# A transformer block with attention and routed experts on one core: pair results in three buffers with a later scatter, a last part reordered around residuals read from PSUM, and early finishing in five steps

## The chip, the core and the metric

The kernel runs on one core of a Trainium2 chip. A core has five engines with queues of their own: TensorE (matmul, "PE"; its weight loads are listed as "PEld"), VectorE ("DVE"), ScalarE ("ACT"), GpSimd ("POOL") and SyncE ("SP", which here only issues DMAs). ACT and POOL issue DMAs too. Each engine works through its instructions in order and waits on semaphores for the others. Matmul results go to PSUM[...]. The metric is device time in microseconds, the median over runs of the same program.

## The reference

The input x has 8 sequences of 512 tokens with 256 features, all fp32. First attention (4 groups of 4 query heads, head size 128, causal), then a feed-forward layer with 64 routed experts and one shared expert. Both are wrapped in layer norms and added to the residual:

```python
x = x + _layernorm(attn(_layernorm(x), wq, bq, wkv, bkv, wo))
x = x + _layernorm(ffn(_layernorm(x), gate_w, w_gate, w_up, w_down, sh_gate, sh_up, sh_down))

# ffn: logits -> softmax -> the best 6 of 64 experts per token
# each expert takes its first 64 tokens, in token order over all sequences
g = silu(einsum('ech,ehf->ecf', buf, w_gate)); u = einsum('ech,ehf->ecf', buf, w_up)
d = einsum('ecf,efh->ech', g * u, w_down)
y = weighted sum of d over the chosen experts
y = y + (silu(x @ sh_gate.T) * (x @ sh_up.T)) @ sh_down.T
```

An expert has 256 inputs and 176 hidden values, the shared expert 352 hidden values. An expert's 64 places are mostly taken by the first sequences.

## The kernel before

The order of instructions on each engine is written out by hand: the Python code emits them in the order in which each engine will do them.

**Attention.** 128 head steps, k = 16 b + s (sequence b, head s). In a step TensorE does the scores of head k (`psc`), the output projection of head k-3 (`po`, accumulated in two PSUM banks o0 and o1 over a sequence), the queries of head k+1 (`pq`, which DVE turns into `qt`) and the mix of head k-2 (`pav`, which ACT copies to `ao`). Between scores and mix, DVE takes the row minimum, ACT the exponential (`e`), DVE the reciprocal of the sum, POOL the multiplication with it ("weigh", L306), DVE and two DMA legs through DRAM the transposition (`eb` to `ex_d` to `et`).

**Feed-forward of sequence b** rides along in sequence b+1's head steps, at fixed places. A place is a letter in the head step: A after weigh, B after the projection, M after the queries, D after the mix. The dictionary `steps` in `feed_forward` names head and place ("7A"). `shared` is the shared expert as a generator: hidden values in three chunks of 128, 128 and 96 columns, taken in the order 2, 1, 0, each as matmuls into two banks (`psg`, `psu`), a tanh on ACT (`gs`) and two DVE operations (`hid`, L692 and L693), and then the 12 products with `sd_sb` (L698). `route` is the router, `output` the last layer norm and residual of a sequence.

**Experts.** The first five sequences (EARLY) write their normalised rows to DRAM. From the end of sequence 5 on, `experts` works off 32 pairs of experts, two calls per pair step, up to four calls per head step: gather of rows by an indirect DMA of POOL (`gx`), weights (`wgu`, `wd`) by DMAs that ACT issues, `gate_up`, `turn_hidden`, `down`. `down` has ACT scale the bank `pd` into `dd` (L584), and POOL scatters `dd` into `y_d` in DRAM with an adding indirect DMA (L585). `dd` comes from a pool of two buffers. Tokens of sequences 5 to 7 that an expert still takes are handled by the "late" pair, with 0/1 matrices instead of an indirect DMA.

**Early finishing.** When all pairs are done, `finish_early` finishes sequences 0 to 4, one step per head step from head 5 of sequence 7 on, at the place before `queries` (L927). `finish` issues two loads of `y_d` and one of the residual `x1_d` from SP, then adds the two (L661, DVE) and goes on into `output`: statistics, scaling on ACT, residual add on POOL, store. A new sequence starts every second step.

**The end.** After head 127, `last_part` does the feed-forward of sequence 7, which nothing rides along with, and in between what is left of sequence 6 (`shared6`, `output6`) and of the early finishing (`spare`). The PSUM banks are three of tag "s", three of tag "m", and o0 and o1.

Of the kernel before, what the change touches and what calls it, by code (L numbers as in the profile page):

```python
# [11 lines left out]
F32 = mybir.dt.float32  # L12
# [32 lines left out]
def sandwich_kernel(ctx, tc, x, wq, bq_t, wkv, bk_t, bv, wo, gate_wt, w_gate, w_up, w_down,  # L45
# [77 lines left out]
    with ExitStack() as part:  # L123
# [446 lines left out]
        def down(key):  # L570
            l = pairs[key] if key == "late" else pairs.pop(key)
            pd = ps_m.tile([P, E], F32, tag="m", name=f"pd_{key}")
            for c in range(2):
                for e in range(2):
                    nc.tensor.matmul(pd[ts(e, CAP), :], lhsT=l["ht"][:, c, ts(e, CAP)],
                                     rhs=l["wd"][:, e, c, :], start=c == 0, stop=c == 1)
            dd = p3.tile([P, E], F32, tag="dd", name=f"dd_{key}")
            if key == "late":
                l["dd"] = dd
                on_act(dd, pd)  # L580
                return
            for e in range(2):
                rows = slice(e * CAP, (e + 1) * CAP)
                nc.scalar.mul(dd[rows, :], pd[rows, :], l["gw"][rows, e : e + 1])  # L584
            nc.gpsimd.indirect_dma_start(  # L585
                out=y_d[:, :], out_offset=bass.IndirectOffsetOnAxis(ap=table["idx"][:, key, 1:2], axis=0),
                in_=dd, in_offset=None, compute_op=ALU.add)
# [32 lines left out]
        def experts():  # L620


            yield from tables()
            yield
            yield from free_slots()
            yield
            for m in range(NM + 5):
                if m < NM:
                    start_pair(m)
                for behind_, step in ((5, down), (3, gate_up), (4, turn_hidden), (2, turn_rows),  # L630
                                      (1, load_gate_up), (3, load_down)):
                    if 0 <= m - behind_ < NM:
                        step(m - behind_)
                yield
                if 0 <= m - 3 < NM:
                    gate_up_hidden(m - 3)
                if m == NM + 4:
                    pairs["all"] = True
                yield
# [14 lines left out]
        def finish(b, tags):  # L654

            ys = [q.tile([P, NI, E], F32, tag=tag, name=f"y{n}_{b}") for n, (q, tag) in enumerate(tags[:2])]
            for k in range(2):
                nc.sync.dma_start(out=ys[k], in_=rows_of(y_d, k * (ET_ROWS + CAP) + b * T))
            x1 = residual(b, *tags[2])
            yield  # L660
            nc.vector.tensor_add(ys[0], ys[0], ys[1])  # L661
            yield from output(b, ys[0], x1)
# [6 lines left out]
        def shared(b, xt2, l, banks="mmmmmm"):  # L669

            hid = p1.tile([P, len(SH_CHUNKS), T], F32, tag="hid", name=f"hid_{b}")
            banks = iter(banks)

            for n, (f0, fw) in reversed(list(enumerate(SH_CHUNKS))):
                mw = min(P, fw + NX // 2)
                pgu = []
                for w_sb, name in ((sg_sb, "psg"), (su_sb, "psu")):
                    tag = next(banks)
                    pp = {"m": ps_m, "s": ps_s}[tag].tile([P, T], F32, tag=tag, name=f"{name}_{b}_{n}")
                    for c in range(NC):  # L680
                        nc.tensor.matmul(pp[:mw, :], lhsT=w_sb[:, c, ds(f0, mw)], rhs=xt2[:, c, :],
                                         start=c == 0, stop=c == NC - 1)
                    pgu.append(pp)
                if fw < P:
                    l["lg"] = p1.tile([NX, T], F32, tag="y", name=f"lg_{b}")
                    on_act(l["lg"][: NX // 2, :], pgu[0][fw:, :])
                    on_act(l["lg"][NX // 2 :, :], pgu[1][fw:, :])

                gs = p2.tile([P, T], F32, tag="gs", name=f"gs_{b}_{n}", bufs=1)
                nc.scalar.activation(gs[:fw, :], pgu[0][:fw, :], AF.Tanh, scale=0.5)  # L690
                yield
                nc.vector.scalar_tensor_tensor(gs[:fw, :], gs[:fw, :], 1.0, pgu[0][:fw, :], ALU.add, ALU.mult)  # L692
                nc.vector.scalar_tensor_tensor(hid[:fw, n, :], gs[:fw, :], 0.5, pgu[1][:fw, :], ALU.mult, ALU.mult)  # L693
                yield
# [6 lines left out]
            if b == B - 1:  # L701
                l["py"] = [ps_o.tile([P, 2, E], F32, tag=f"o{n}", name=f"py_{b}_{n}") for n in range(2)]
                for i in range(NI):
                    products(i, l["py"][i // 2][:, i % 2, :], i % 2 == 0, False)
                yield
                return
# [14 lines left out]
        def feed_forward(b):  # L721
# [79 lines left out]

            steps["shared"], steps["output"] = go("f"), lambda: next(l["out"]) if "out" in l else begin_output()
            return steps

        def last_part(before, spare):
# [4 lines left out]
            shared6, output6 = before["shared"], before["output"]  # L810
            shared6()
            mv, rs = norm_scales([sums[i // 2][:, i % 2, :] for i in range(NI)], f"o{b}")
            shared6()
            shared6()
            shift = shifts(mv, rs, f"o{b}")
            two = p2.tile([P, 2, NI * E], F32, tag="v", name="o_xt2")
            o, xt2 = two[:, 0].rearrange("p (i e) -> p i e", i=NI), two[:, 1].rearrange("p (c t) -> p c t", c=NC)
            st = small.tile([P, NI, 6], F32, tag="st", name=f"st_f{b}")
            for i in range(NI):
                scale_on_act(o[:, i, :], sums[i // 2][:, i % 2, :], rs, shift, i)  # L820
                nc.vector.tensor_add(xt[:, i, :], xt[:, i, :], o[:, i, :])
                nc.vector.bn_stats(st[:, i, :], xt[:, i, :])
            mv, rs = scales_of(st, NI, f"f{b}")
            shared6()
            shift = shifts(mv, rs, f"f{b}")
            nc.sync.dma_start(out=rows_of(x1_d, b * T), in_=xt)
            xg = p1.tile([P, NI, ROW], F32, tag="xg", name=f"xg_{b}")
            for i in range(NI):
                if i % 2:
                    scale_on_act(xg[:, i, :E], xt[:, i, :], rs, shift, i)  # L830
                else:
                    normalize(xg[:, i, :E], xt[:, i, :], mv, rs, i)
            transpose_rows(xt2, xg, f"f{b}")
            f = shared(b, xt2, l, "msmsms")
            next(f)
            r = route(b, xg, l)
            for _ in spare:
                pass
            next(r)
            shared6()  # L840
            next(r)
            next(r)
            next(r)
# [5 lines left out]
            next(f)  # L849
            gate_up("late")  # L850
            next(f)
            gate_up_hidden("late")
            next(f)
            turn_hidden("late")
            next(f)
            down("late")
            py = l["py"]
# [3 lines left out]
            shared6()  # L861
            output6()
            output6()
# [5 lines left out]
            shift = shifts(mv, rs, f"y{b}")  # L869
            for i in range(NI):  # L870
                scale_on_act(o[:, i, :], py[i // 2][:, i % 2, :], rs, shift, i)
                nc.vector.tensor_add(xt[:, i, :], xt[:, i, :], o[:, i, :])  # L872
                if i % 2:
                    nc.sync.dma_start(out=rows_of(out, b * T)[:, i - 1 : i + 1, :], in_=xt[:, i - 1 : i + 1, :])
            output6()
# [4 lines left out]
        def finish_early():  # L880
            rows = [finish(b, EARLY_TAGS + [[(p1, "xn"), (p2, "xnt")][b % 2]]) for b in range(EARLY)]
            yield
            for t in range(2 * EARLY + 2):
                for b in range(EARLY):
                    if 0 <= t - 2 * b < 4:
# [22 lines left out]
        for k in range(NK):  # L908
# [50 lines left out]
            if twice and not finishing:  # L959
                next(routed, None)  # L960
# [92 lines left out]
```

## Time and profile before

| what | us |
|---|---|
| median of 3 runs (1465.49 to 1471.9) | 1470.83 |
| the profiled execution | 1466.5 |
| its span, first to last instruction | 1464.8 |
| TensorE busy / DVE / ACT / POOL | 1405.2 / 890.4 / 509.7 / 427.8 |
| expert pairs, first `pd` to last scatter | 1005 to 1290 |
| early finishing, first load to last add | 1297 to 1389 |
| last part, end of the last projection to the last DVE instruction | 1399.8 to 1453.0 |
| last DMA issue | 1453.9 |

Times in the trace are counted from the start of the span. A timeline line has start, length, engine, code line, operation, output and inputs with their shapes, and in brackets the idle time of that engine just before and what ended it. Operations of one kind in a row are merged, with their count as x4. A matmul of fp32 appears as two records. Busy time of TensorE is modelled, and matmuls overlap, so that the distance between starts says more than the length. A line of windows has the stretch, its length, the busy time of PE, PEld, DVE, ACT and POOL with the number of instructions, the granted TensorE clock as a share of full speed, the busy share of the DMA engines and GB/s.

### The profile page before, as it was taken

The page shows a single profiled execution, that of the slowest core. Times are in us where ns is not written, and L with a number is a line of the kernel's source. Part 1 is how long each engine was busy: PE and PEld are TensorE (multiplying, and loading weights), DVE is VectorE, ACT ScalarE, POOL GpSimd, SP SyncE. Part 2 cuts the span into 40 slices and gives each one's busy share as a digit, 9 for nine tenths or more (in the row PEclk, how much of TensorE's full clock was granted, in tenths as well). Part 3 has the DMA queues.
Part 4 walks back from the last instruction along what each step waited for, and adds up shares of the span by engine and source line. Part 5 has one row for each costly group of instructions (what it writes and reads, how often), then busy time and mean ns, then how long its engine had stood idle before and what let it go on. Part 6 is the DMA issues. An engine that isn't in the chain of part 4 may idle for free. (4 is left out here: it accounts for less than half of the span.)

```text
span 1464.8 us, 18561 instructions
## 1 busy us (share of the span) xinstructions
PE 1405.2 (96%) x5310; PEld 854.5 (58%) x5310; DVE 890.4 (61%) x3094; ACT 509.7 (35%) x1450; POOL 427.8 (29%) x682
## 2 busy tenths in 40 slices
PE   9999999999999999999999999989999999998985
PEld 5665665666565665666565656655545655555653
DVE  5565576657755676557665676576465444577643
ACT  2333343234422433234323442233332333444432
POOL 2222232124211232123112421134344353444311
PEclk9999999999999999999999999999999999999998
DMA  7664464355544554346435554459998889868711
GB/s 257 195 201 142 145 185 132 108 153 169 156 129 131 161 169 139 118 149 184 139 97 156 169 165 126 122 180 245 265 254 239 234 225 252 203 190 245 239 47 63
DMA packets 160790, 252.03 MB, mean 172 GB/s; under 512 B 16412, under 2 KB 136189, under 8 KB 160685
## 3 DMA queue, kind: packets, MB, share of 16 engines
q1 hardware_dynamic: 131149, 206.76, 47.1%
q10 hardware_dynamic: 23392, 34.61, 8.5%
q0 software_dynamic: 6144, 9.44, 3.4%
q8 instruction: 44, 0.72, 0.2%
q14 instruction: 61, 0.50, 0.1%
HBM read 143.01 MB, written 107.74 MB: 171 GB/s over the span
## 5 line engine op out<-in xcount | busy, mean ns | idle before, releaser
L306 POOL TENSOR_SCALAR e<-e,recip 128x128 f32<-128x128 f32 x508 | 271.7, 578 | 788.8 <-DVE recip L303 760.6
L296 ACT ACTIVATE e<-e,least 128x128 f32<-128x128 f32 (+3 forms) x512 | 285.8, 559 | 363.8 <-DVE least L293 330.9
L289 PE MATMUL psc<-kt,qt 128*128 128x128 f32 (+3 forms) x1024 | 309.0, 440 | 13.9 <-DVE qt L279 6.6
L349 PE MATMUL pav<-et,v 128*128 128x512 f32 (+3 forms) x1024 | 298.1, 434 | 4.4 <-ACT dd L584 3.6
L349 PEld LDWEIGHTS pav<-et,v 128*128 128x128 f32 x1024 | 193.7, 190 | 165.8 <-issue 115.9
L293 DVE CUSTOM_DVE_ANT_0 e<-psc,mask 128x128 f32<-128x128 f32 (+3 forms) x512 | 232.7, 479 | 70.5 <-PE psc L289 63.1
L361 PE MATMUL po<-wo_sb,ao 128*128 128x256 f32 x1024 | 244.2, 382 | 0.7 <-ACT ao L109 0.7
L276 PE MATMUL pq<-xnt,wq_sb 128*128 128x512 f32 x512 | 242.1, 595 | 0.2 <-ACT sc L388 0.2
L361 PEld LDWEIGHTS po<-wo_sb,ao 128*128 128x128 f32 x1024 | 193.8, 191 | 72.8 <-issue 41.2
L322 DVE STREAM_TRANSPOSE eb<-e 128x128 f32<-128x128 f32 x756 | 227.7, 364 | 6.1 <-DMA ex_d<-eb 6.0
L109 ACT COPY ao<-pav 128x512 f32<-128x512 f32 x128 | 75.0, 586 | 419.6 <-PE pav L349 395.5
L289 PEld LDWEIGHTS psc<-kt,qt 128*128 128x128 f32 x1024 | 165.8, 190 | 91.0 <-issue 21.0
L279 DVE SCALAR_TENSOR_TENSOR qt<-pq,bq_sb,pe_sb 128x512 f32<-128x512 f32 x128 | 95.5, 746 | 95.8 <-PE pq L276 95.8
L276 PEld LDWEIGHTS pq<-xnt,wq_sb 128*128 128x128 f32 x512 | 96.2, 191 | 70.1 <-issue 64.1
L303 DVE RECIPROCAL recip<-total 128x4 f32<-128x4 f32 x128 | 22.8, 178 | 123.4 <-ACT e L296 122.4
L296 ACT ACTIVATION_READ_ACCUMULATOR e<-e,least 128x1 f32 x512 | 95.7, 187 | 0.0
L585 POOL DMA_INDIRECT y_d<-dd,idx x32 | 51.3, 1603 | 123.6 <-DMA y_d<-dd,idx 90.5
L248 PE MATMUL pk<-xnt,wkv_sb 128*128 128x512 f32 x128 | 60.3, 594 | 0.2 <-ACT xnt L109 0.2
L259 PE MATMUL pv<-wkv_sb,xnt 128*128 128x512 f32 x128 | 59.1, 593 | 0.0
L261 DVE TENSOR_TENSOR v<-pv,bv_sb 128x512 f32<-128x512 f32 x32 | 22.1, 691 | 60.8 <-PE pv L259 60.8
L112 DVE COPY ht<-pth 88x256 f32<-88x256 f32 x32 | 13.4, 418 | 66.8 <-PE pth L566 55.3
L251 DVE SCALAR_TENSOR_TENSOR kt<-pk,bk_sb,pe_sb 128x512 f32<-128x512 f32 x32 | 24.0, 750 | 47.4 <-PE pk L248 47.4
(193 smaller groups left out, 1123.2 us busy)
## 6 DMA issues: line engine op xcount, KB each, us to landing
ex_d<-eb SPq DMA_DIRECT2D x126, 640.0 KB
et<-ex_d SPq DMA_DIRECT2D x504, 160.0 KB
wgu<-in_w_gate ACTq DMA_DIRECT2D x32, 352.0 KB
wgu<-in_w_up ACTq DMA_DIRECT2D x32, 352.0 KB
wd<-in_w_down ACTq DMA_DIRECT2D x32, 352.0 KB
y<-y_d SPq DMA_DIRECT2D x10, 512.0 KB
x<-in_x SPq DMA_DIRECT2D x8, 512.0 KB
x_d<-x SPq DMA_DIRECT2D x8, 512.0 KB
```

The source lines that it names most:

```text
L109: nc.scalar.copy(dst, src)
L248: nc.tensor.matmul(pk, lhsT=wkv_sb[:, c, g, 0, :], rhs=s["xnt"][:, c, :], start=c == 0, stop=c == NC - 1)
L259: nc.tensor.matmul(pv, lhsT=s["xnt"][:, c, ts(i, P)], rhs=wkv_sb[:, c, :, 1, :], start=c == 0, stop=c == NC - 1)
L276: nc.tensor.matmul(pq, lhsT=wq_sb[h // QPG][:, c, ts(h % QPG, D)], rhs=seqs[b]["xnt"][:, c, :], start=c == 0, stop=c == NC - 1)
L279: nc.vector.scalar_tensor_tensor(qt, pq, bq_sb[:, h : h + 1], pe_sb, ALU.add, ALU.add)
L289: nc.tensor.matmul(psc[:, :w], lhsT=l["qt"][:, ts(i, P)], rhs=seqs[b]["kt"][h // QPG][:, :w], start=True, stop=True)
L293: nc.vector.tensor_tensor_reduce(out=e, in0=psc[:, :w], in1=mask[:, T - w :], scale=-1.0 / math.sqrt(D), scalar=BIG, op0=ALU.add, op1=ALU. ...
L296: nc.scalar.activation(e, e, AF.Exp, bias=l["least"][:, i : i + 1], scale=-1.0, accum_out=l["total"][:, i : i + 1])
L306: engine.tensor_scalar(e, e, recip[:, n : n + 1], 1.0, ALU.mult, ALU.mult)
L322: nc.vector.transpose(blocks.rearrange("p c j t -> p j c t"), l["e"][i][:, js[0] * P : (js[-1] + 1) * P].rearrange("p (j c t) -> p j c t", ...
L349: nc.tensor.matmul(pav[:, :, j:, :], lhsT=seqs[b]["v"][:, j, ts(g, D)], rhs=l["et"][:, :, AT[j] : AT[j] + NI - j, :], start=j == 0, stop=j ...
L361: nc.tensor.matmul(po[b][i // 2][:, i % 2, :], lhsT=ao[:, ts(i, P)], rhs=wo_sb[:, h, :], start=h == 0 and i % 2 == 0, stop=h == NH - 1, sk ...
```

## The change

The diff does several things at once. Pairs' results: `dd` gets three buffers, and its scatter is issued in the second half of a pair step, after `gate_up_hidden`, no longer in `down`. Early finishing: the loads of `y_d` are issued from ACT, the load of `x1_d` becomes a step of its own (five steps per sequence in place of four), and in heads 12 and 14 of sequence 7 a second step is done at the end of the head step. Last part: the residual of sequence 7 is made by DVE straight from the projection's banks, without the shift, which POOL adds to it later; the products of sequences 6 and 7 are cut in three parts (`part`) that stand between other matmuls, sequence 6's accumulate in o0 and o1; sequence 6's `output` moves in front of the last products; the last residual is a subtraction of the mean and a multiply-add on DVE.

```diff
-            l = pairs[key] if key == "late" else pairs.pop(key)
+            l = pairs[key]
...
-            dd = p3.tile([P, E], F32, tag="dd", name=f"dd_{key}")
+            dd = l["dd"] = p3.tile([P, E], F32, tag="dd", name=f"dd_{key}", bufs=3)
...
+        def scatter(m):
             nc.gpsimd.indirect_dma_start(
-                out=y_d[:, :], out_offset=bass.IndirectOffsetOnAxis(ap=table["idx"][:, key, 1:2], axis=0),
-                in_=dd, in_offset=None, compute_op=ALU.add)
+                out=y_d[:, :], out_offset=bass.IndirectOffsetOnAxis(ap=table["idx"][:, m, 1:2], axis=0),
+                in_=pairs.pop(m)["dd"], in_offset=None, compute_op=ALU.add)
...
                     gate_up_hidden(m - 3)
+                if 0 <= m - 5 < NM:
+                    scatter(m - 5)
...
-                nc.sync.dma_start(out=ys[k], in_=rows_of(y_d, k * (ET_ROWS + CAP) + b * T))
+                nc.scalar.dma_start(out=ys[k], in_=rows_of(y_d, k * (ET_ROWS + CAP) + b * T))
+            yield
             x1 = residual(b, *tags[2])
...
+            def part(py, n):
+
+                fw = SH_CHUNKS[n][1]
+                for i in range(NI):
+                    nc.tensor.matmul(py[i // 2][:, i % 2, :], lhsT=hid[:fw, n, ts(i, P)], rhs=sd_sb[:fw, n, :],
+                                     start=n == 2 and i % 2 == 0, stop=False, skip_group_check=True)
+
+            def late(py):
+                l["y"] = p1.tile([P, NI, E], F32, tag="y", name=f"y_{b}")
+                for i in range(NI):
+                    nc.tensor.matmul(py[i // 2][:, i % 2, :], lhsT=l["gt"][:, ts(i, P)], rhs=l["dd"], start=False,
+                                     stop=True, skip_group_check=True)
+                    if i % 2:
+                        on_act(l["y"][:, i - 1 : i + 1, :], py[i // 2])
+                nc.sync.dma_start(out=rows_of(ly_d, b * T - ET_ROWS), in_=l["y"])
...
-                gs = p2.tile([P, T], F32, tag="gs", name=f"gs_{b}_{n}", bufs=1)
+                gs = (p2.tile([P, T], F32, tag="qt", name=f"gs_{b}_{n}") if b == B - 2 and n == 0 else
+                      p2.tile([P, T], F32, tag="gs", name=f"gs_{b}_{n}", bufs=1))
...
-            for i in range(NI):
-                scale_on_act(o[:, i, :], sums[i // 2][:, i % 2, :], rs, shift, i)
-                nc.vector.tensor_add(xt[:, i, :], xt[:, i, :], o[:, i, :])
+
+            for i in range(NI):
+                nc.vector.scalar_tensor_tensor(xt[:, i, :], sums[i // 2][:, i % 2, :], rs[:, i : i + 1], xt[:, i, :],
+                                               ALU.mult, ALU.add)
                 nc.vector.bn_stats(st[:, i, :], xt[:, i, :])
+            shift = shifts(mv, rs, f"o{b}")
+            py6 = [ps_o.tile([P, 2, E], F32, tag=f"o{n}", name=f"py_{b - 1}_{n}") for n in range(2)]
+            other["part"](py6, 2)
             mv, rs = scales_of(st, NI, f"f{b}")
-            shared6()
-            shift = shifts(mv, rs, f"f{b}")
-            nc.sync.dma_start(out=rows_of(x1_d, b * T), in_=xt)
+            other["hidden"](0)
+            fshift = shifts(mv, rs, f"f{b}")
...
+            other["hidden"](1)
             transpose_rows(xt2, xg, f"f{b}")
+            for i in range(NI):
+                nc.gpsimd.tensor_scalar(xt[:, i, :], xt[:, i, :], shift[:, i : i + 1], 1.0, ALU.add, ALU.mult)
+            nc.sync.dma_start(out=rows_of(x1_d, b * T), in_=xt)
+            other["part"](py6, 0)
             f = shared(b, xt2, l, "msmsms")
             next(f)
+            other["part"](py6, 1)
             r = route(b, xg, l)
-            for _ in spare:
-                pass
             next(r)
-            shared6()
+            other["late"](py6)
             next(r)
             next(r)
+            next(f)
+            next(f)
             next(r)
...
             gate_up("late")
             next(f)
+            py = l["py"] = [ps_o.tile([P, 2, E], F32, tag=f"o{n}", name=f"py_{b}_{n}") for n in range(2)]
+            l["part"](py, 2)
+            l["part"](py, 1)
             gate_up_hidden("late")
-            next(f)
             turn_hidden("late")
-            next(f)
+            l["part"](py, 0)
             down("late")
-            py = l["py"]
+            output6()
+            output6()
+            output6()
...
-            shift = shifts(mv, rs, f"y{b}")
-            for i in range(NI):
-                scale_on_act(o[:, i, :], py[i // 2][:, i % 2, :], rs, shift, i)
-                nc.vector.tensor_add(xt[:, i, :], xt[:, i, :], o[:, i, :])
+            for i in range(NI):
+                nc.vector.tensor_scalar(o[:, i, :], py[i // 2][:, i % 2, :], mv[:, i, 0:1], None, ALU.subtract)
+            for i in range(NI):
+                nc.vector.scalar_tensor_tensor(xt[:, i, :], o[:, i, :], rs[:, i : i + 1], xt[:, i, :],
+                                               ALU.mult, ALU.add)
...
-            for t in range(2 * EARLY + 2):
+            for t in range(2 * EARLY + 3):
...
-                    if 0 <= t - 2 * b < 4:
+                    if 0 <= t - 2 * b < 5:
...
+            if finishing and s in (12, 14):
+                next(routed, None)
```

For sequence 6, `shared` makes its chunks' hidden values only when `hidden(n)` is called (chunk 2 as before), and it has no products of its own any more; for sequences 6 and 7 `part` and `late` do them.

## The prediction

> **What bounds the kernel now.** The profiled execution took 1466.5 us, 1464.8 of them span. I read the page first (TensorE 1405.2 us busy, 96%), then the waits of TensorE, then windows and timelines where it idles. Nearly everywhere matmuls follow without a gap, so only a stretch where TensorE stands, or runs at a reduced clock, can give time back. Waits, by columns "who waited on whom: us in total, times, longest"; the first two lines are TensorE's in 1000-1290 us (the expert stretch), the last two are of ACT and POOL in the whole span:
>
> ```profile
> PE pd L575 <- DMA wd<-in_w_down: 8.0, 6, 2.9
> PE pav L349 <- ACT dd L584: 3.6, 4, 1.8
> ...
> POOL y_d L585 <- DMA y_d<-dd,idx: 90.5, 16, 8.1
> ACT dd L584 <- DMA y_d<-dd,idx: 28.2, 9, 7.2
> ```
>
> Each scatter waits on POOL for the one before to land; with two dd buffers ACT then waits too, but only 3.6 us of that reach TensorE. Windows of the last part (us, busy time by engine, granted clock, DMA) show the big hole:
>
> ```profile
> 1399.80:1406.70 6.90, 6.89 (x17) 2.71 (x15) 3.23 (x12) 2.29 (x5) 1.01 (x1) 1.00 0.00 0
> 1406.70:1411.70 5.00, 0.00 (x0) 0.00 (x0) 4.76 (x17) 1.12 (x3) 1.01 (x1) 1.00 0.31 107
> 1411.70:1415.00 3.30, 3.25 (x10) 2.23 (x11) 0.98 (x3) 1.29 (x3) 0.00 (x0) 0.51 0.02 5
> ```
>
> TensorE is empty for 5 us while DVE makes the residual, then runs at half clock. The timeline (start, length, operation, idle before) tells what it waits for, and how the part ends:
>
> ```profile
> 1405.51 1.93 ACT L97 ACTIVATE o_xt<-po,shift_o,rs_o 128x256 f32<-128x256 f32 x4
> 1406.10 0.42 DVE L821 TENSOR_TENSOR x<-x,o_xt 128x256 f32<-128x256 f32 x1 [2.04 <-ACT o_xt L97]
> ...
> 1411.20 0.73 DVE L106 TENSOR_SCALAR xg<-x,mv_f,rs_f 128x256 f32<-128x256 f32 x2
> ...
> 1444.29 1.08 PE L575 MATMUL pd_late<-wd_late,ht_late 88*64 88x256 f32 x8
> ...
> 1451.16 1.80 DVE L872 TENSOR_TENSOR x<-x,o_xt 128x256 f32<-128x256 f32 x4 [0.63 <-ACT o_xt L97]
> ...
> 1453.45 0.45 SPq L651 DMA_DIRECT2D out_dram<-x  x1
> ```
>
> **The last part: 8.9 us, and 0.4 behind it.** First residual: the four ACT scalings leave the chain. rs_o is ready at 1402.2 (POOL 1401.19 + 1.01). The new bank-reading add is priced at 0.42 (L692 takes 0.68 for 512 columns from a bank, L558 0.34 for 176); with statistics one pair runs at L821/L822's pitch, 0.79. So 1402.3 + 3.15 = 1405.4 in place of 1409.3. Then aggregate and eps 0.6, POOL power 1.0, shift, xg on ACT 1.1; the two hidden(0) operations of sequence 6 (1.4) fit under the power: xg at 1409.0 (was 1412.4).
>
> [...] Rows: 128x256 from a bank (L418) 0.425, SBUF to SBUF (L872) 0.426. [...] by the rows they cost nothing. I take the rows.
>
> TensorE meanwhile gets sequence 6's products, 12 matmuls, 24 records at 0.216 = 5.2 us, in thirds: one at 1406.5-1408.2 (banks free at 1405.4), one after the transposes (1409.4-1411.1, hiding the two copies of xt2), one after the first 3.4 us chunk of sequence 7 (1411.1-1414.5), hiding the lg copies. Forward with rows' durations, before -> after: that chunk 1418.1 -> 1414.5; router exponentials (ACT, no longer behind y's scalings) 1422.4 -> 1418.7; chosen, 3.3 us of DVE, 1425.8 -> 1422.0; place counts 1426.2 -> 1422.8 (TensorE idles 0.8, as they need the bank that hidden(2) reads); gather ends 1432.4 -> 1428.5, both remaining chunks being in front of it; gate_up 1430.5; two product thirds 1434.0; turn 1434.3; last third 1436.0; pd_late ends 1445.4 -> 1437.1; last matmul 1447.8 -> 1439.3. Check: these matmuls stream for some 37.4 us; before they took 47.8, by this 39.3.
>
> Tail: statistics 1.6, aggregate 0.6, to 1440.95. The mean is subtracted in 1.7 under the power, whose start POOL's four adds for sequence 6 (2.8, released by ACT from 1438.2) delay to 1441.7; four adds, 1.8: end 1444.5 (was 1453.0). I put 0.4 on the shorter end: the last issue is a 256 KB half, where 512 KB came last. From last SP issue to last SP issue, 1453.9 -> 1445.0: 8.9. Bounds: 6, if two 1 us waits I don't see enter a schedule with only 2 us slack, and 10.
>
> At nothing: four POOL shifts (L649's 2.8 for four) with the x1 store behind them, read only 30 us later; gs in qt's ring, last read before 1384; y_6's banks, copied by 1419.9 and wanted at 1430.5. Uncovered, the POOL shifts cost at most 2.8.
>
> **Pairs: 2.9 us.** A third dd buffer lets dd(m) wait for scatter m-3. The scatters still go one by one (21 to 29: 70.6 us, 8.8 each, against 8.0 for a pair on TensorE), but the deadline moves a pair back; the half step later takes 4 us of that. ACT's holds go. TensorE's four stalls were 0.35, 0.33, 1.13, 1.81: the first two run into a wait for wd (DMA share near 1), which absorbs them; at 1250 and 1265 the next weights had landed 1 us or more ahead. So 2.94; ends 0 and 3.6. On POOL weigh and the next gather queue behind the moved scatter; weigh's reciprocal comes 10 us after the previous scatter's place, about when that lands: no charge, and the transposes that want weigh come a head later.
>
> **Early finishing: 1.9 us.** Loads go to ACT, one step ahead of x1's load and two ahead of the add, so DVE's 6.4 us of waits for y (4 times) vanish. The add plus statistics (1.23 + 1.41 + 0.36 + 0.17 = 3.1 us) still stand before qt. I model a stall as DVE work between reciprocal and qt less the head's slack (its matmul time minus 6.0): it gives 0.9 against 0.8 seen at 1371 and 2.1 against 2.0 at 1350:
>
> ```profile
> 1348.56 1.23 DVE L661 TENSOR_TENSOR y<-y,y 128x1024 f32<-128x1024 f32 x1 [2.80 <-DMA y<-y_d]
> ...
> 1352.41 0.38 PE L289 MATMUL psc<-kt,qt 128*128 128x128 f32 x1 [1.87 <-DVE qt L279]
> ```
> ```profile
> 1352.40:1355.40 3.00, 2.99 (x8) 1.76 (x9) 2.33 (x10) 1.09 (x4) 0.41 (x1) 0.72 0.96 228
> 1355.40:1358.40 3.00, 3.00 (x10) 2.28 (x9) 2.01 (x9) 1.43 (x4) 0.59 (x2) 0.71 1.03 382
> ```
>
> Before: stalls of 1.1, 1.8, 2.0, 0.8, 0.6 for the gt copy behind y's scalings, and 1.8 of reduced clock (6 us at 0.72) = 8.1. After, adds in heads 8, 10, 12, 13 and at the end of 14: 1.0, 1.85 (marks stand there too), 1.3, 0.1, 1.1 = 5.35, plus the clock. [...] here 1.87 us did, while 1.66 at 1328 did not. [...] by the row 3.65; it lies at the edge, so half: 0.9. 8.1 - 6.25 = 1.9; ends -1 and +4. Ten issues of 0.4-0.5 us on ACT, busy 35 to 64% here, lie in its idle time before the ao copies.
>
> **Sum.** 8.9 + 0.4 + 2.9 + 1.9 = 14.1: the profiled 1466.5 would be 1452.4. The median shown, 1470.83, lies 4.3 above that execution; taking the gain from it gives **1456.7**, 1.0% faster. About 0.5% (7.4 us) can be told from no change.
>
> **Rivals.**
> 1. *Hidden outside the last part* (0.25): freed ACT only meets full DMA (wd waits 8.0 us, more than dd's), and the crowding of adds into heads 12 to 14 takes back what the loads give. Only 9.3 or less: 1461.5, and 1464 with the lower bound. For: DMA share about 1 in much of the expert stretch. Against: none of the wd waits follows the 1.81 stall.
> 2. *More: loads come earlier too* (0.12): dd's holds of ACT, 28.2 us, also hold the weight issues behind them. If half of the 8.0 goes, with 2 of the half-clock time after the 2.9 us wait: 6 more, 1450.5. Against: at 1052.98 and 1228.62 the wd issue stood until another transfer landed, not for dd.
> 3. *Slower: ACT held by its new loads* (0.06). A load that cannot be issued stops ACT, and behind it stand the ao copy and the next exponentials, which psc and project await. It has happened:
>
> ```profile
> 1229.04 0.40 ACT L296 ACTIVATE e<-e,least 128x128 f32<-128x128 f32 x1 [6.37 <-DMA wgu<-in_w_up]
> ```
>
> Five pairs at 6.4 + 6.4 (one hold each load), less 3 free, with 1.8 of clock: 5 x 11.6 = 58, net +44: 1515. The point is about 4.1 us held per pair, (h - 3 + 1.8) x 5 = 14.1. Against: that row had DMA share 0.99 and three loads in a row; from 1300 the share is 0.47 to 1.01, and the buffers are freed a step earlier.
> 4. *The thirds don't fill the hole* (0.05), a bank or hid's single buffer holding them: then about 4 from the chain alone, 2.9 and 1.9: 1462.
>
> My forecast has 0.52. The low end, 1448, reaches rival 2 with spread; the high end, 1465, rival 1 with the last part at 6. Faster 0.85; same 0.09 (rivals 1 and 4 at their worst); slower 0.06.
>
> **What would show it.** No empty 5 us before the xg transposes and clock 1.00 after; residual adds from banks at 0.42; pd_late about 8 us sooner against the last project; no dd wait on y_d in ACT's list; no DVE wait for y. I am wrong if ACT's list shows waits at the y loads, if wd waits grow by what dd's lost, or if the head with the marks stalls 3 us.

## The result, and the profile after

| | before | after | ratio after/before, 95% interval |
|---|---|---|---|
| with the prediction | 1469.78 us (11 runs) | 1456.37 us (11 runs) | 0.9917 [0.9893, 0.9941] |
| measured once more | 1467.83 us (11 runs) | 1458.18 us (6 runs) | 0.9939 [0.9926, 0.9952] |
| profiled span | 1464.8 us | 1454.6 us | |

The change makes the kernel 0.6 to 0.8% faster, 9 to 12 us by the two ratios. 1456.7 us had been forecast. That number was met, but the two ratios lie above the forecast one (1456.7 / 1470.83 = 0.9904; only the first interval holds it), and the sum behind it was right in one term, near in another and of the wrong sign in a third. This table shows it. It is read from one trace for each column: the time from the start of head step 105 (counted from 0 over all 128; 112 is head 0 of sequence 7) to that of 118, where the last pairs end; from there to the end of the last projection, where the early finishing lies; and the last part to the end of DVE. A head step starts with its first `psc`. The last line counts from the end of the issue.

| us | before | after | after, once more | predicted gain |
|---|---|---|---|---|
| head step 105 to 118 (pairs) | 211.1 | 208.3 | 210.8 | 2.9 |
| 118 to the end of the last projection (finishing) | 110.9 | 114.5 | 112.6 | 1.9 |
| last part | 53.1 | 44.2 | 44.2 | 8.9 |
| last SP issue to the end of the span | 10.9 | 10.0 | 10.1 | 0.4 |

**Last part.** The windows of the changed kernel's last part (us, busy time of TensorE, weight loads, DVE, ACT, POOL; granted clock, DMA share, GB/s) and then its timeline (start, length, operation, idle before):

```profile
1399.50:1404.00 4.50, 4.50 (x12) 1.98 (x11) 3.18 (x12) 0.60 (x1) 1.02 (x1) 1.00 0.02 4
1404.00:1408.00 4.00, 4.00 (x15) 2.38 (x13) 3.79 (x15) 1.11 (x3) 1.13 (x2) 1.00 0.01 2
1408.00:1411.00 3.00, 2.94 (x18) 2.40 (x18) 2.08 (x4) 1.17 (x3) 1.80 (x4) 1.00 0.08 28
```
```profile
1401.96 0.48 DVE L847 SCALAR_TENSOR_TENSOR x<-po,rs_o,x 128x256 f32<-128x256 f32 x1 [1.13 <-POOL rs_o L87]
1402.48 0.43 DVE L849 BATCH_NORM_STATS2 st_f<-x 128x6 f32<-128x256 f32 x1
...
1406.25 1.89 PE L682 MATMUL py<-sd_sb,hid 96*128 96x256 f32 x8
...
1407.37 0.73 DVE L106 TENSOR_SCALAR xg<-x,mv_f,rs_f 128x256 f32<-128x256 f32 x2
...
1407.98 1.42 PE L119 MATMUL pt_f<-ident,xg 128*128 128x128 f32 x8
```

The hole of 5 us in which TensorE stood, and the half clock behind it, are gone: TensorE is busy throughout at 1.00. A third of sequence 6's products (L682) stands where the hole was, and the bank-reading add needs no scaling on ACT.

**Pairs and finishing.** TensorE's waits after (who waited on whom: us, times, longest), first in 1000-1290 us, then in 1290-1460, and POOL's in the whole span:

```profile
PE pd L575 <- DMA wd<-in_w_down: 8.3, 4, 4.3
...
PE psc L289 <- DVE qt L279: 2.1, 1, 2.1
```
```profile
PE psc L289 <- DVE qt L279: 3.8, 3, 1.5
PE pav L349 <- DMA et<-ex_d: 3.4, 1, 3.4
DVE eb L322 <- DMA ex_d<-eb: 2.8, 1, 2.8
```
```profile
POOL y_d L586 <- DMA y_d<-dd,idx: 85.6, 16, 8.2
```

ACT's wait of dd for a scatter (28.2 us before) is no longer in the list. One wait is longer and one is new. psc of head 118 stands 2.1 us (0.8 before) for the qt that DVE makes in head step 117; this is called the stall of head step 117 from here on. And one pav, in head 14 of sequence 7 (head step 126), stands 3.4 us for transposed exponentials. Both cost clock as well in this trace. SP's timelines, before and in the changed kernel, show where the second comes from; then TensorE's in the changed kernel, and its windows:

```profile
1353.41 0.39 SPq L651 DMA_DIRECT2D out_dram<-x  x1
1355.55 0.34 SPq L326 DMA_DIRECT2D ex_d<-eb  x1
...
1361.88 0.51 SPq L666 DMA_DIRECT2D x<-x_d  x1
```
```profile
1353.77 2.44 SPq L329 DMA_DIRECT2D et<-ex_d  x3
1356.31 0.39 SPq L654 DMA_DIRECT2D out_dram<-x  x1
1361.54 0.38 SPq L670 DMA_DIRECT2D x<-x_d  x1
1362.02 0.44 SPq L326 DMA_DIRECT2D ex_d<-eb  x1
```
```profile
1374.39 4.60 PE L349 MATMUL pav<-et,v 128*128 128x512 f32 x8 [3.40 <-DMA et<-ex_d]
```
```profile
1371.00:1374.40 3.40, 0.01 (x1) 0.04 (x1) 2.52 (x9) 2.47 (x7) 0.96 (x3) 0.90 1.07 278
1374.40:1379.00 4.60, 4.60 (x9) 2.78 (x10) 3.38 (x10) 1.03 (x3) 4.60 (x6) 0.50 0.59 215
```
```profile
1373.75:1380.50 6.75, 6.11 (x13) 4.05 (x14) 4.52 (x14) 2.76 (x7) 6.41 (x9) 0.50 0.75 237
```

Before, the load of x1 (L666) came 8.5 us behind the store (L651) that reads the same buffer, with an ex_d between them. Now it (L670) stands right behind the store (L654), so SP waits 4.8 us for the store to land. ex_d, whose transposes were done at 1359.2, stands behind both and is issued at 1362.02. pav then waits 3.40 us, and its eight matmuls take 4.60 us at clock 0.50 in place of 2.39. The half clock lasts until 1380.5, so that it costs some 3.1 us behind the wait, 6.5 us with it.

### The profile page after: what moved, and what is told of

The parts are those of the page before. It is cut to its first block, busy times and chain, and to the rows that moved or that the text cites. A ratio compares the mean times of both kernels' runs of the same rounds, so it can differ in the third digit from the quotient of the medians.

```text
span 1454.6 us, 18553 instructions
## 1 busy us (share of the span) xinstructions
PE 1403.1 (96%) x5310; PEld 855.2 (59%) x5310; DVE 892.8 (61%) x3097; ACT 505.8 (35%) x1442; POOL 429.2 (30%) x686
## 5 line engine op out<-in xcount | busy, mean ns | idle before, releaser
L306 POOL TENSOR_SCALAR e<-e,recip 128x128 f32<-128x128 f32 x508 | 274.1, 597 | 787.0 <-DVE recip L303 749.1
L322 DVE STREAM_TRANSPOSE eb<-e 128x128 f32<-128x128 f32 x756 | 228.1, 365 | 8.6 <-DMA ex_d<-eb 6.4
```

The lines of the kernel that those rows point to most:

```text
L306: engine.tensor_scalar(e, e, recip[:, n : n + 1], 1.0, ALU.mult, ALU.mult)
L322: nc.vector.transpose(blocks.rearrange("p c j t -> p j c t"), l["e"][i][:, js[0] * P : (js[-1] + 1) * P].rearrange("p (j c t) -> p j c t", ...
```

## The experiments

Each kernel is timed beside the kernel before, with the ratio to it; the stage times are from its trace, in the order of the second table (105 to 118 / 118 to last projection / last part). Each run left one trace.

**Pairs undone.** Two dd buffers, scatter in `down`, all else as changed:

```diff
-            dd = l["dd"] = p3.tile([P, E], F32, tag="dd", name=f"dd_{key}", bufs=3)
+            dd = l["dd"] = p3.tile([P, E], F32, tag="dd", name=f"dd_{key}")
...
                 nc.scalar.mul(dd[rows, :], pd[rows, :], l["gw"][rows, e : e + 1])
+            scatter(key)
...
-                if 0 <= m - 5 < NM:
-                    scatter(m - 5)
```

> The changed kernel with the pairs' part alone undone (two dd buffers, scatter issued in down again). In the profile of the changed kernel head step 116 starts 5.2 us earlier than before (1265.9 against 1271.1), more than the 2.9 I had priced. If that comes from dd's third buffer and the later scatter, this run starts head step 116 at 1270 to 1272, shows TensorE waits on ACT dd of 3 to 4 us again, and takes 3 to 5 us more than the changed kernel. If full DMA queues are the bound there and the 5.2 us are chance of one execution, head step 116 starts at 1264 to 1268 again and the time is within 2 us of the changed kernel's.

1458.93 us, ratio 0.9946 [0.9926, 0.9967]; stages 211.3 / 113.8 / 44.2. Its waits in 1000-1290 us:

```profile
ACT dd L583 <- DMA y_d<-dd,idx: 26.5, 7, 6.5
...
PE pav L349 <- ACT dd L583: 4.6, 3, 2.4
```

ACT's holds are back, 4.6 us of them reach TensorE, and the first stage is the old one.

**Finishing undone.** Loads of y on SP again, four steps a sequence, no second slots, and the loop over what is left restored in the last part:

```diff
-                nc.scalar.dma_start(out=ys[k], in_=rows_of(y_d, k * (ET_ROWS + CAP) + b * T))
-            yield
+                nc.sync.dma_start(out=ys[k], in_=rows_of(y_d, k * (ET_ROWS + CAP) + b * T))
...
-                    if 0 <= t - 2 * b < 5:
+                    if 0 <= t - 2 * b < 4:
...
-            if finishing and s in (12, 14):
-                next(routed, None)
```

> The changed kernel with the early finishing alone undone (loads on SP with the x1 load beside them, four steps per sequence, no second step in heads 12 and 14; the fifth sequence's last two steps stand in the last part). From the start of head step 116 to the end of the last projection the changed kernel's profile needs 133.7 us, the one before 128.7. If the early finishing lost these 5 us, this run needs 128 to 130 and is 3 to 6 us faster than the changed kernel. If the forecast was right that it gains 1.9 us and one profile is no measure, this run is 1 to 4 us slower.

1455.75 us, ratio 0.9919 [0.9897, 0.9941]; stages 208.3 / 111.7 / 44.2. No wait of pav on et after 1290. The time cannot be told from the changed kernel's; the stage is 0.9 to 2.8 us shorter. The new finishing brings nothing that can be measured.

**Last part undone.** The kernel before with the pairs and the finishing of the change.

> The kernel before with the pairs' part and the early finishing of the change, but the old last part. If the last part is worth what the forecast says and the profiles show (9.3 us from the last projection to the last issue, 10.2 with what lies behind it), this run takes 9 to 11 us more than the changed kernel, so that it is 2 to 5 us faster than the kernel before or not to be told from it. If the last part is worth 6 us or less, the rest of the change has to give 6 us or more against the kernel before. Its head step 126 has the same wait of 3 to 4 us on et if that wait belongs to the early finishing.

1467.1 us, ratio 0.9994 [0.9979, 1.001]; stages 208.7 / 114.7 / 53.0. The windows show the hole again:

```profile
1409.00:1414.20 5.20, 0.15 (x2) 0.14 (x1) 4.96 (x17) 1.32 (x4) 1.01 (x1) 0.96 0.38 133
1414.20:1418.00 3.80, 3.80 (x12) 2.31 (x13) 0.76 (x2) 1.14 (x3) 0.00 (x0) 0.60 0.29 100
```

Pairs and finishing together are worth nothing that can be measured; the last part carries the whole gain.

**x1 loaded one step later**, in the step of the add, so that a load of x1 no longer meets the store of its own buffer (that of sequence 3 is issued 11.9 us after it):

```diff
-            x1 = residual(b, *tags[2])
             yield
+            x1 = residual(b, *tags[2])
             nc.vector.tensor_add(ys[0], ys[0], ys[1])
```

> The changed kernel with the load of x1 moved one step later, to the step that adds y's halves; nothing else. Theory one: the 3.4 us wait for et in head step 126 (with some 2.5 us of reduced clock behind it) comes from SP, where the x1 load of sequence 3 stands until the store of sequence 1 from the same buffer has landed, with ex_d of that head behind it. Then this run loses the wait: TensorE's wait on et in 1290 to 1400 us under 0.7, from head step 116 to the last projection 127 to 129 us in place of 133.7, time 4 to 6 us less than the changed kernel. Theory two: the two y loads from ACT, 1 MB just before, fill the DMA engines, and ex_d lands late wherever SP issues it. Then the wait stays at 2 to 4 us and the time is within 1.5 us of the changed kernel's.

1456.27 us, ratio 0.9928 [0.9906, 0.995]; stages 208.9 / 112.1 / 44.2. SP's timeline over the same store; the load behind it is now that of sequence 2, into the other buffer:

```profile
1356.66 0.40 SPq L654 DMA_DIRECT2D out_dram<-x  x1
1359.16 0.38 SPq L670 DMA_DIRECT2D x<-x_d  x1
1359.64 0.45 SPq L326 DMA_DIRECT2D ex_d<-eb  x1
```

ex_d goes out 2.4 us earlier and pav's wait falls from 3.40 to 0.79 us. It is SP's queue that held it, since the loads of y are still issued from ACT here. But one head later a wait of 1.81 us for DVE's least appears, and the time is unchanged within the interval.

**Third buffer only**, and **later slot only.** The changed kernel with the scatter back in `down`, and with two dd buffers, each alone.

> The changed kernel with three buffers for a pair's result, but each scatter issued where it was before, right behind the scalings. Theory 1 (the third buffer alone frees ACT; the later slot only puts a scatter in front of weigh of head 116): no wait of ACT dd in the expert stretch reaches TensorE, head 116 begins at 1264 to 1266 us as in the changed kernel, the stall of head 117 falls from 2.1 to 1.1 us or less and its 2 us of lowered clock go; 116 to the end of the last projection 130 to 132 us in place of 133.7; time 1453.5 to 1456. Rival (the later slot does the work, since it lets gate_up of a later pair and its loads go first): head 116 at 1268 to 1271 us; time 1457 to 1460.

> The changed kernel with the scatters in their later slot, but two buffers for a pair's result as before. Theory 1 (the buffer is what counts): dd of a pair now waits for a scatter that was issued half a step later still, so ACT's holds are longer than before's 1.81 us at their longest (3 to 6 us) and reach TensorE; head 116 begins at 1271 to 1278 us; the stall of head 117 stays at 2 us; time 1459 to 1466. Rival (the slot counts, not the buffer): head 116 at 1265 to 1268 us; time 1455 to 1457.5.

Buffer only: 1458.74 us, 0.9921 [0.9896, 0.9946]; 210.5 / 113.8 / 44.2. Slot only: 1460.85 us, 0.9943 [0.9925, 0.9961]; 210.5 / 112.2 / 44.2. With two buffers, dd's waits are back (22.9 us, longest 6.7), so the buffer frees ACT. But half of my theory fell: without the later slot the stall of head step 117 did not fall to 1.1 us, it rose. POOL, then TensorE, in the run with the buffer only:

```profile
1278.72 1.57 POOL L587 DMA_INDIRECT y_d<-dd,idx  x1 [3.04 <-DMA y_d<-dd,idx]
1279.74 2.62 POOL L306 TENSOR_SCALAR e<-e,recip 128x128 f32<-128x128 f32 x4
```
```profile
1288.46 2.42 PE L289 MATMUL psc<-kt,qt 128*128 128x128 f32 x8 [2.57 <-DVE qt L279]
```

The scatter stands in front of weigh (L306) in either slot. What changed is when TensorE comes. The last scatters go one by one, each waiting for the one before to land (83.7 us of such waits in 1000-1290 us of this run, 7.9 at the longest), and weigh of head step 116 is at the end of that chain. In the kernel before, weigh also stood behind that chain (until 1280.19 us), but ACT's holds delayed TensorE too, so that only 0.81 us showed.

**Finishing spread out.** One finishing step in each of two slots of every head, and the add and the statistics of a sequence in two heads:

```diff
-            yield
             nc.vector.tensor_add(ys[0], ys[0], ys[1])
+            yield
...
-            for t in range(2 * EARLY + 3):
+            for t in range(24):
                 for b in range(EARLY):
-                    if 0 <= t - 2 * b < 5:
+                    if t in ([20, 21, 22, 23] if b == 4 else [4 * b + 4, 4 * b + 6, 4 * b + 7, 4 * b + 8]) or t == max(4 * b, 2):
                         next(rows[b])
...
-            if finishing and s in (12, 14):
+            if finishing:
                 next(routed, None)
```

> The changed kernel with early finishing spread out: one step in each of two slots of every head from 105-th-head accounting on (it was four slots in two heads besides the first slot), and the add and the statistics of a sequence in two heads in place of one, so that no head's VectorE work before qt takes more than 1.94 us, under the slack of 2.0. The load of x1 stands a head behind the store that frees its buffer. Theory (crowding of VectorE and SP's wait for a store are what the finishing loses): no wait of pav on et, stalls of psc on qt of 1.0 us or less but for head 117's 2.1, no lowered clock but there; head 116 to the end of the last projection 125 to 128 us in place of 133.7; time 1449 to 1453. Rival (the stalls come from DMA latency of the transposed exponentials under y's loads, or from ACT behind its new loads): stalls of the same sum stand at other heads, 131 to 134 us; time 1455 to 1458.

1449.02 us, ratio 0.9874 [0.9843, 0.9904]; stages 208.6 / 106.4 / 44.2. TensorE's waits in 1290-1400 us:

```profile
PE pav L349 <- DMA et<-ex_d: 2.2, 3, 0.9
...
PE psc L289 <- DVE qt L279: 0.4, 1, 0.4
```

3.8 us of waits for qt have become 0.4 and none of these is longer than 0.9. The theory holds in the main, though 2.2 us of waits for et remain where none had been expected: with the same work and the same transfers, only their places differ, and the stage is 6 to 8 us shorter than in the two profiles of the changed kernel.

**Spread, and third buffer with the early scatter.**

> The finishing spread out as in the run before, together with three buffers and the scatters in their former slot. Theory: the two gains add up: head 116 begins at 1264 to 1266 us, head 117 stalls 1.1 us or less, 116 to the end of the last projection 122 to 126 us, last part 44.2 us; time 1446 to 1451, the lowest of all. Rival (the later slot matters for the expert stretch): head 116 at 1268 to 1271 us, and the time no lower than that of the run with the spread alone.

1452.36 us, ratio 0.9878 [0.9852, 0.9904]; stages 209.2 / 111.9 / 44.3. The gains do not add up: head step 117 stalls 2.55 us, and one pav waits 4.0 us for et again. There SP's store (1368.68) and load of x1 (1370.42) stood until two loads of y, issued on ACT at 1360.10 and 1360.56, had landed (see the last section), and ex_d, ready at 1367.33, went out behind them at 1370.90. So spread steps do not always keep SP free. In time the run cannot be told from the one before.

**Weigh ahead of the scatter** where both meet (head steps 113 to 116), on top of the spread finishing:

```diff
-                    scatter(m - 5)
+                    due.append(m - 5)
...
             weigh(k)
+            scatter_due()
```

> The run with the finishing spread out, and one order changed on POOL: where a scatter fell right in front of a head's weigh (heads 113 to 116), weigh now goes first. Theory (the stall at head 117 is POOL's chain of scatters, each waiting for the one before to land, with weigh of head 116 at its end; it shows wherever the third buffer lets TensorE come early, whatever the scatter's slot): DVE's eb of head 116 no longer waits for weigh and takes 1.8 us in place of 2.4; the stall of head 117 falls from 1.81 to 0.6 to 1.0 us; head 116 to the end of the last projection 123 to 125 us against 125.0; time within 2 us of the run before it, 1447 to 1451. Rival (the stall is DVE's own work for the last pair, not POOL): it stays at 1.6 to 2 us.

1451.54 us, ratio 0.9902 [0.9883, 0.992]; stages 211.2 / 108.1 / 44.2. The transposes (L322) of head 116 on DVE, in the changed kernel and then here; TensorE here, and its waits in 1000-1290 us:

```profile
1277.28 2.42 DVE L322 STREAM_TRANSPOSE eb<-e 128x128 f32<-128x128 f32 x6 [1.01 <-POOL e L306]
```
```profile
1278.98 1.81 DVE L322 STREAM_TRANSPOSE eb<-e 128x128 f32<-128x128 f32 x6
```
```profile
1286.04 2.43 PE L289 MATMUL psc<-kt,qt 128*128 128x128 f32 x8 [0.35 <-DVE qt L279]
```
```profile
PE pd L575 <- DMA wd<-in_w_down: 6.7, 4, 3.0
PE ptx L538 <- DMA gx<-xg_d,idx: 5.1, 2, 2.6
```

The stall of head step 117 fell to 0.35 us with POOL's order alone, and the transposes no longer wait for weigh: it started at 1276.10, while the scatter now behind it could not start before 1280.01, as the one before had to land. So the stall is POOL's chain and not DVE's work. (TensorE came to head step 117 at 1277.77 us here; in three runs with the old order where it came at 1277.0 to 1277.9 it stalled 0.84, 0.89 and 2.57.) But the scatters start later behind weigh, and the gathers of the next pairs, behind them on POOL, make TensorE wait 5.1 us that were not there.

**Loads of y half a head apart**, on top of that.

> The run with weigh ahead of the scatter, and the two 512 KB loads of y of a sequence half a head apart instead of back to back. The eight DMA semaphores are taken in turn over SP and ACT, so an issue stands until the DMA eight before it has landed; in the run with the finishing spread out the store at 1364.3 and the load of x1 at 1366.7 stood so behind the two loads of y issued at 1358.6 and 1359.1, and ex_d of the head behind them. Theory: with the loads apart each lands sooner (4 us in place of 5.7 and 7.6), ex_d is issued within 1 us of its transposes, and no wait of pav on et over 0.5 us is left from 1290 on (three of 2.2 us in all before); head 116 to the end of the last projection 121 to 124 us; time 1445 to 1449. Rival (the loads land no sooner, since the queues are shared with marks and rows of the last sequences): waits of pav on et of 2 us or more in all remain; time as before.

1455.53 us, ratio 0.9907 [0.989, 0.9923]; stages 215.8 / 108.8 / 44.2. The rival holds for et: 3.0 us of waits of pav on et remain (3.1 in the run before), and the stage is no shorter. The waits for gathered rows were 8.5 us here, so what moving weigh costs differs from run to run.

**The changed kernel once more.**

> The changed kernel as it is, on the chip and in the rounds of the two runs above, to compare with them: 1454 to 1458 us, a stall of pav on et in head 126 of 3 to 4 us and of psc on qt in head 117 of 2 us or more; by the theory 6 to 9 us above the run with weigh ahead of the scatter.

1458.18 us, ratio 0.9939 [0.9926, 0.9952]; stages in the second table. pav waited 3.6 us for et again, but head step 117 stalled only 0.89: a wait of 4.4 us for wd at 1233 had made TensorE late before it got there. Two traces of one kernel so differ by 2.5 and 1.9 us in the first two stages, which bounds what a single stage time tells.

**Last scatter only.**

> The run with the finishing spread out, and of the scatters only the last one put behind a weigh, that of head 116. In the run with all four moved the stall of head 117 had gone (0.35 us), but the gathers of the pairs before stood on POOL behind the delayed scatters and TensorE waited 5.1 us for their rows. Theory: no gather is queued behind the last scatter, so those 5.1 us are not paid: no wait of ptx on gx, head 116 at 1266 to 1268 us, stall of head 117 under 1 us, head 116 to the end of the last projection 123.5 to 125.5 us; time 1446 to 1450, within 2 us of the run with the finishing spread out alone. Rival (the waits for gathered rows come from run to run, not from the order): ptx waits again, head 116 at 1269 us or later, time 1451 or more.

1451.43 us, ratio 0.9883 [0.9863, 0.9903]; stages 208.0 / 105.4 / 44.2. The edit missed: the last scatter is issued at the end of head step 116 and not in front of its weigh, so the order of instructions on every engine stayed that of the run with the finishing spread out. It tells nothing of its theory; it is a second measurement of that run, and the second to lie 17 us or more below the kernel before.

## Why the prediction was right in its time and wrong in one term

**The last part: 8.9 us predicted, 8.9 found** (53.1 to 44.2, and 53.0 with it undone). The single steps hold, counted from the end of the last projection: the last pd_late ends at 37.1 us (predicted 37.3), DVE at 44.2 (44.7). The bank-reading multiply-add (L847) took 0.47 us, not 0.42. The rows that I had priced it by held all the same: L907 of the changed kernel, the same operation on 256 columns with every operand in SBUF, takes 0.48, and the statistics of 256 columns take 0.42 from a bank (L77, st_o) and 0.41 to 0.43 from SBUF (L77, st_y, and L849). So no cost of the bank above 0.02 us shows here; the 0.05 us lie between a multiply-add and the plain adds before (0.41 to 0.43). Behind the last part 0.9 us came where 0.4 was put.

**Pairs: 2.9 predicted, 2.1 found.** Three traces with two buffers (before, pairs undone, slot only) took 211.1, 211.3 and 210.5 us from head step 105 to 118; seven with three buffers and the later slot 208.0 to 210.8, on average 208.8. In the times alone so little does not show. The mechanism was right, with the step "weigh behind the moved scatter: no charge" mis-sized. The reciprocal came not "about when that lands" but 4 us earlier: at 1272.3, while weigh started at 1276.28 behind a scatter that had waited for its predecessor. The stall of head step 117 is 0.8 to 2.6 us long in the seven traces, 1.5 on average, against 0.7 in the three with two buffers; the difference is as large as the 0.8 missing from 2.9. Over all 14 traces it follows one number, how long after the start of head step 117 weigh of head 116 starts: with 0.2 us or less either way the stall is 0.6 to 0.9, with 0.7 to 0.8 it is 1.5 to 1.7, with 1.3 it is 2.1, with 1.8 to 1.9 it is 2.6, and where weigh starts 1.7 and 3.8 us ahead, 0.35 and 0.17. The deadline of ACT moved back by a pair, but not that of POOL, whose chain of scatters ends in the same place. Two traces with three buffers and the early slot took 210.5 and 209.2 us, so the later slot may be worth 1 us of the 2.1; two do not settle it. Part of rival 1 is also seen: the waits for wd did not shrink (8.0 before, 8.3 after).

**Early finishing: +1.9 predicted, with -1 as its lower end; -2.7 found** (113.6 us on average over six traces with the new finishing, that is after, after once more, pairs undone, last part undone, buffer only and slot only, against 110.9 before). Against 111.7 in the trace with the finishing undone it is -1.9. This is the step that failed. The stalls that I had worked out from DVE's slack came as put: 1.0, 1.85 and 1.3 us predicted for heads 8, 10 and 12, and in the trace psc started 1.02, 1.68 and 1.57 us later than its usual 0.11 us behind the start of the matmul before it (0.86, 1.52 and 1.40 as idle time). The waits of DVE for y did vanish, and ACT was not held by its loads (rival 3; its list of waits in 1290-1384 us has none for a DMA). What I had not counted is the queue that I did not look at: the second slot puts the load of x1 right behind the store of the sequence two before, which has the same buffer, and SP then holds every ex_d and et behind it. Where I had put 0.1 us for head 13 and 1.1 for head 14, pav waited 3.4 us in one go. That wait, of 3.4 to 3.95 us, is in all six of these traces and in neither of the two with the old finishing.

TensorE's waits of over 0.3 us from the start of head step 118 on add up to 8.4 to 9.0 us in the six traces, against 6.2 before and 5.7 with the finishing undone; I had forecast 5.35 in place of 6.3. So some 2.5 us of idle time came where 1 was to go, and that is most of the 2.7. The clock, of which I had expected 0.9 (half of 1.8, an estimate from the gaps of 1.87 and 1.66 us before), follows no order by kernel: in this stretch the six traces have none to three pieces of half clock of 3.4 us each, before had one, and the finishing undone two.

Loading x1 later took 2.6 us of the wait away, which shows what pav had waited for; other waits came in its place, and the sum stayed at 8.4. Spreading the steps brought the sum to 3.0 to 5.6 us and the stage to 105.4 to 108.8 in four traces; in the fifth, with the early scatter, it was 7.2 and 111.9. So the place of the steps, more than the loads themselves, is what costs, though slow loads still reached SP in the fifth.

**The sum.** 8.9 + 0.9 + 2.1 - 2.7 = 9.2 us, against 14.1; the ratios give 9.0 and 12.2. The profiled spans differ by 10.2 with 1.2 of it before head step 105, whose start scatters from 1074.9 to 1080.8 us over the 14 profiles without any order by kernel. That the forecast time was met to 0.3 us is therefore partly chance: the gain was put 2 to 5 us too high, and 1470.83, from which it was taken, lies 1 to 3 us above every later median of the kernel before. A slip in rival 2 changes nothing: 6 us below 1456.7 is 1450.7.

A version that beats both was measured: the changed kernel with its finishing spread out, twice, 0.9874 [0.9843, 0.9904] and 0.9883 [0.9863, 0.9903], by the ratios 17 to 19 us below the kernel before and 5 to 10 us below the change. Its intervals overlap the first of the change's two by 0.001 and lie clear of the second.

Left open: a kernel with the last scatter alone behind weigh was not run, and why splitting the loads of y did not help et was not settled.

## What to carry to other kernels

When a step moves to a new slot, write down for each queue what then stands directly in front of what: here a load behind the store that frees its buffer stood for 4.8 us on SP and stopped everything behind it, even what belonged to another part of the kernel (one pav waited 3.40 us). When a third buffer frees one engine, ask which other chain kept the same pace unseen: here the scatters on POOL took over as soon as TensorE came earlier (the stall of head step 117 grew from 0.7 to 1.5 us on average). The same work in smaller pieces, each below the slack that I had estimated for one head (2.0 us), gained more here than moving two loads to another engine: ratios of 0.9874 and 0.9883 against 0.9917 and 0.9939.

## What the hardware showed that I had not expected

The clock after a gap did not follow the gap's length. Windows of the changed kernel, then of the run with the buffer only, both around the stall of head step 117; then of the run with the later slot only, around its wait of pav for et:

```profile
1282.00:1285.00 3.00, 0.91 (x5) 0.57 (x3) 2.91 (x10) 0.58 (x1) 3.00 (x6) 1.00 0.37 46
1285.00:1288.70 3.70, 3.69 (x8) 2.47 (x9) 2.30 (x10) 1.09 (x4) 1.43 (x2) 0.54 1.08 286
```
```profile
1285.50:1288.40 2.90, 0.39 (x3) 0.19 (x1) 2.87 (x10) 0.58 (x1) 2.90 (x6) 1.00 0.35 63
1288.40:1292.00 3.60, 3.54 (x14) 2.61 (x15) 2.88 (x14) 1.10 (x4) 1.49 (x2) 1.00 1.11 277
```
```profile
1375.20:1379.20 4.00, 0.06 (x1) 0.02 (x1) 3.12 (x12) 2.36 (x6) 0.85 (x3) 1.00 1.04 261
1379.20:1383.00 3.80, 3.70 (x14) 2.24 (x14) 3.73 (x13) 1.73 (x4) 3.80 (x5) 1.00 0.54 212
```

A gap of 2.10 us was followed by clock 0.54 for 3.7 us; one of 2.57 us by 1.00, and even one of 3.95 us by 1.00. So in these runs the length alone did not decide it, since 2.10 us cost clock and 3.95 did not, and the edge near 1.87 us, which was my estimate from two gaps, did not hold either. What is the same in all 14 traces, the last 30 us of the span apart, is the size: the granted clock is whole or half, and the half clock comes in pieces of 3.4 us, or 6.8 for two in a row. In the trace of the changed kernel the pieces begin at 988.0, 1237.2 and 1285.0 us (3.41 each) and at 1063.1 and 1373.7 (6.83 each). So the 6 us at 0.72 that the prediction shows are one such piece of 3.4 us, from 1353.7 on, among full clock. What decides whether a gap draws one was not found.

The length of a merged line is not always work. The six transposes of head 116 take 1.81 us in one line shown above and 2.42 us in the other. In the longer one they follow weigh's four pieces (1276.28 to 1278.89 us): three of the four with 256 columns stood 0.14, 0.10 and 0.02 us for theirs, idle times too short to be printed, and took 0.45 us in place of 0.40. Of the 504 transposes of 256 columns in that trace only three more took 0.45, at 1268.3 to 1269.5 us, behind weigh in the same way; the other 498 took 0.39 to 0.41 us, 31 of them while POOL computed.

By the semaphore numbers in the trace of the changed kernel, the 829 DMAs of SP and ACT share eight completion semaphores (100 to 106 and 109) in turn, 103 or 104 each, and 346 of the issues name their own semaphore among those that they wait for. So an issue can also stand for the DMA that had its semaphore before, though that uses another buffer: an et issue on SP, with semaphore 101, stood 1.24 us and went out at 1355.43, when the load of y that ACT had issued at 1350.75, with 101 too, had landed (1355.41). In the run with the finishing spread out the load of x1 at 1366.70 carried the semaphore of a load of y issued on ACT at 1359.09:

```profile
1364.34 0.88 SPq L654 DMA_DIRECT2D out_dram<-x  x1
1366.70 0.38 SPq L670 DMA_DIRECT2D x<-x_d  x1
1367.18 0.45 SPq L326 DMA_DIRECT2D ex_d<-eb  x1
```

It stood 1.5 us, and ex_d behind it.
